# Order of blends, border rows, side work and weight buffers in a deformable-convolution and mixture-of-experts kernel

## The chip, the cores and the metric

The kernel runs on one core of a Trainium2 chip. The metric is the device time of one execution in microseconds (us); the time stated for a kernel is the median of its runs. The profile that the text reads is that of one execution.

## What is computed

The input is `x`, four images of 256 channels and 64 x 64 pixels, in float32. The reference normalises each pixel over its channels, and then applies three modulated deformable 3 x 3 convolutions, each with a ReLU. For every pixel and each of nine taps, a plain 3 x 3 convolution gives an offset (dy, dx) and a mask; the input is sampled at the shifted place by bilinear blending of four neighbours, and the samples are multiplied with a 256 x 256 weight per tap.

```python
om = lax.conv_general_dilated(x, w_off, ...) + b_off[None, :, None, None]
off = om[:, :2 * K].reshape(B, K, 2, H, W)
mask = jax.nn.sigmoid(om[:, 2 * K:])
...
sampled = _bilinear(x, ys, xs) * mask[:, None]
out = jnp.einsum('bikhw,oik->bohw', sampled, wk) + b[None, :, None, None]
```

The result is added to `x`. Each of the 4 x 4096 pixels is then a token of 256 values. A token is normalised, a gate picks two of eight experts, and each expert is a two-layer network (256 to 512, GELU, 512 to 256) with biases. The two experts' results, weighted by the gate, are added to the token.

## The kernel before

**Tiling.** An image is cut into eight blocks of 512 pixels (eight rows of 64). A stage is one layer of one image; `self.stages` in `run` lists the twelve stages in a fixed order, chosen so that, but for two places, a stage does not need the one just before it. `main_block` walks one block: nine taps (`k`), and for each tap two pairs of 128-pixel groups (`t0`).

**Main path of a pair.** `samples` issues, for each of the two groups, an indirect gather from a table in DRAM (L503, on POOL, that is GpSimd) into a tile `g` of `self.gat`. One gathered row per pixel holds the four neighbours. VectorE (DVE in the profile) blends the two columns (L509, 128 x 512), then the two rows (L514, 128 x 256, into a tile `s`, of which there are eight), and ScalarE (ACT) scales the result by mask and weights (L517). `turn` works `LAG` = 2 pairs behind: four TensorE (PE) transposes (L532) and an ACT copy out of PSUM (L535). `finish` follows one tap behind that: the matmuls with the tap's weights (L555). After the ninth tap ACT writes the block (L577), for layers 0 and 1 into a window `win` of ten rows (eight and a border row on each side), for layer 2 into `r`.

**Side work.** Python generators hold the rest: `store_table` writes a window's rows into the DRAM table of the next layer; `off_block` computes offsets and masks of a block (PE matmuls L357 over the window, then some twelve small DVE instructions, L395 and after, that make the gather's indices and the blend's factors); `pre_block` normalises the next image; `tokens` forms, stores and normalises tokens and ranks the experts. `aside` puts a generator into a list once for each of its steps; `step(k)`, called after each tap, runs as many entries from the list's front as will empty it by the end of the block. Border rows that lie outside of the image are zeroed by memsets when a window is taken (L290, L292).

**Experts.** Three lanes (`routes`, `tiles`, `sums`) run beside the taps at a set pace (`Group.pace`; 5, 5, 2, 1.5 taps for one expert step). `expert` yields after each piece: first the bias addition of the step before (`products`, L892 on DVE, `y`) and transposes of 256 gathered tokens; then the first products and GELU (`ph` L856, L866); then `fetch_next` and the second products (`py` L874). `fetch` issues an indirect load of an expert's weights (L800, `w`, 1.18 MB: 128 x 2308 float32) into one of the tiles of `self.w`, and two of tokens (L812, `zt`), all on POOL. If the same buffer already holds the right weights, the row index lies out of bounds and nothing is loaded; `Group.order` therefore gives each buffer its own run of consecutive tiles. After the last tap the lanes are drained (`drain`).

**Order.** Each engine works its queue in order. The framework's scheduler sorts the instructions at build time, by readiness and by the order in which the program makes them. `with self.after(x)` forbids that what is made inside goes ahead of `x` on the same engine. `self.last` is the newest row blend, `self.gathered` the newest gather.

Of the kernel before, what the change touches and what calls it, by code (L numbers as in the profile page):

```python
# [11 lines left out]
ALU = mybir.AluOpType  # L12
# [5 lines left out]
CC = C // P  # L18
# [4 lines left out]
NB = H * W // BLK  # L23
RPB = BLK // W
# [5 lines left out]
Q = 32  # L30
# [4 lines left out]
FT_LOG = 8  # L35
FT = 1 << FT_LOG
FU = FT // P
GB = 10
LAG = 2
LEAST = 2.0**-30  # L40
WINN = CC * (RPB + 2) * W
# [41 lines left out]
class Group:  # L83


    def __init__(self, b, n0, n1):
        self.b, self.n0, self.n1 = b, n0, n1
        self.nm = f"{b}_{n0}"
        self.M = (n1 - n0) * TPB

        self.NF = 2 * self.M * P // FT + E - 1


        self.half = (self.NF + 1) // 2
        self.zt, self.acc, self.gy, self.sums, self.py = {}, [], [], [], None
        self.order = [s // 2 + s % 2 * self.half for s in range(self.NF)]


class Lane:
# [18 lines left out]
class Weave:  # L118
# [3 lines left out]
    def __init__(self, ctx, tc, ins, out):  # L122
        nc = self.nc = tc.nc
        self.tc = tc
        self.ins = ins
        self.x = ins["x"].rearrange("b (c p) h w -> b p c (h w)", p=P)
        self.out_v = out.rearrange("b (c p) h w -> b p c (h w)", p=P)
        self.B = self.x.shape[0]

        def pool(name, bufs, **kw):  # L130
            return ctx.enter_context(tc.tile_pool(name=name, bufs=bufs, **kw))

        self.cst = pool("cst", 1)
        self.dram = pool("dram", 1, space=bass.MemoryType.DRAM)
        self.wkp = pool("wkp", 1)
        self.plan = pool("plan", 19)
        self.win = pool("win", 3)
        self.wt = pool("wt", 2)
        self.small = pool("small", 1)
        self.big = pool("big", 2)  # L140
        self.ffn = pool("ffn", 2)
        self.rt = pool("rt", 1)
        self.rt2 = pool("rt2", 2)
        self.gyp = pool("gyp", 4)
        self.smT = pool("smT", 2)
        self.smp = pool("smp", 8)
        self.gat = pool("gat", GB)
        self.ps = pool("ps", 3, space=bass.MemoryType.PSUM)
        self.ps1 = pool("ps1", 1, space=bass.MemoryType.PSUM)

        self.routes, self.tiles, self.sums = Lane(), Lane(), Lane()
        self.side, self.plans_side = [], []
        self.last = self.gathered = self.turned = None
        self.starting, self.draining, self.later = True, False, []
        self.pend, self.pairs = None, []
# [125 lines left out]
    def window(self, n, nm, spare):  # L281

        if spare:
            if n % 2 == 0:
                self.spare = self.wt.tile([P, 2, WINN], F32, tag="wt", name=f"win_{nm}")
            w = self.spare[:, n % 2, :].rearrange("p (c r w) -> p c r w", c=CC, w=W)
        else:
            w = self.win.tile([P, CC, RPB + 2, W], F32, tag="win", name=f"win_{nm}")
        if n == 0:
            self.nc.vector.memset(w[:, :, 0, :], 0.0)  # L290
        if n == NB - 1:
            self.nc.vector.memset(w[:, :, RPB + 1, :], 0.0)  # L292
        return w

    def rows_done(self, l, b, n, wins):

        nc = self.nc
        w = wins[n]
        if n > 0:
            nc.scalar.copy(w[:, :, 0, :], wins[n - 1][:, :, RPB, :])  # L300
            nc.scalar.copy(wins[n - 1][:, :, RPB + 1, :], w[:, :, 1, :])  # L301
        if l > 0:
            self.aside(3, self.store_table(l, b, n, w))
        ready = [n - 1] * (n > 0) + [n] * (n == NB - 1)
        for m in ready:
            gen = self.off_block(l, b, m, wins[m])
            if self.starting and m >= NB // 2:

                self.later.append(gen)
            else:  # L310
                self.aside(6, gen, True)

    def store_table(self, l, b, n, w):

# [30 lines left out]
    def off_block(self, l, b, n, w):  # L345
# [4 lines left out]

        po = self.ps1.tile([P, BLK], F32, tag="po", name=f"po_{nm}")

        terms = [(ky, kx, c) for kx in (1, 0, 2) for ky in range(3) for c in range(CC)]
        for m, (ky, kx, c) in enumerate(terms):
            g = m % NQ
            x0, x1 = max(0, 1 - kx), min(W, W + 1 - kx)
            nc.tensor.matmul(  # L357
                po[g * Q : (g + 1) * Q, :].rearrange("q (r w) -> q r w", w=W)[:, :, x0:x1],
                lhsT=self.wo[l][:, 3 * ky + kx, c, :],
                rhs=w[:, c, ky : ky + RPB, x0 + kx - 1 : x1 + kx - 1],  # L360
                start=(m < NQ),
                stop=(m + NQ >= len(terms)),
                tile_position=(0, g * Q),
            )
# [26 lines left out]
        nc.scalar.copy(pos.rearrange("p (t k) d -> p t (k d)", k=K), pm[:, :, : 2 * K])  # L391
        yield
        yield
        with self.after(self.last):
            nc.vector.tensor_tensor(  # L395
                pos, pos, self.base[:, n].rearrange("p t k d -> p (t k) d"), ALU.add
            )
# [31 lines left out]
    def pre_block(self, b, n, wins, spare):  # L429
# [8 lines left out]
        for t0 in range(0, TPB, 2):  # L438
# [7 lines left out]
                    )  # L446
            nc.scalar.copy(h[:, t0 : t0 + 2, :], tp)
        yield
        rest = normalise(nc, self.small, h, h, EPS_C, nm)
        with self.after(self.last):  # L450
            next(rest)
# [42 lines left out]
    def samples(self, i, n, k, t0, plan):  # L494


        nc = self.nc
        idx, cf = plan
        ss = []
        for t in (t0, t0 + 1):  # L500
            j = t * K + k
            g = self.gat.tile([P, 2, 2, C], F32, tag="g", name=f"g_{i}_{n}_{j}")
            self.gathered = nc.gpsimd.indirect_dma_start(  # L503
                out=g.rearrange("p x s f -> p (x s f)"),
                out_offset=None,
                in_=self.table(*self.stages[i]),
                in_offset=bass.IndirectOffsetOnAxis(ap=idx[:, j : j + 1], axis=0),
            )
            nc.vector.scalar_tensor_tensor(  # L509
                g[:, :, 0, :], g[:, :, 1, :], cf[:, j, 0:1], g[:, :, 0, :],  # L510
                ALU.mult, ALU.add,
            )
            s = self.smp.tile([P, C], F32, tag="s", name=f"s_{i}_{n}_{j}")
            self.last = nc.vector.scalar_tensor_tensor(  # L514
                s, g[:, 1, 0, :], cf[:, j, 1:2], g[:, 0, 0, :], ALU.mult, ALU.add
            )
            nc.scalar.activation(s, s, AF.Copy, scale=cf[:, j, 2:3])  # L517
            ss.append(s)
        return ss
# [21 lines left out]
    def finish(self):  # L541
# [36 lines left out]
        if l < NL - 1:  # L578
            self.rows_done(l + 1, b, n, wins)
        else:  # L580
            self.aside(7, self.tokens(b, n, r))

# [2 lines left out]
    def tokens(self, b, n, r):  # L587
# [37 lines left out]
        nc.scalar.copy(lg, lp)  # L625
        nc.sync.dma_start(self.t_dram[b][n], tok)
        yield
        rest = normalise(nc, self.small, tok, z, EPS_T, nm)
        with self.after(self.last):
            mean = next(rest)  # L630
# [29 lines left out]
        )  # L660
        nc.scalar.activation(lg, lg, AF.Exp)
        yield
        sm = small("sm", (P, TPB))
        with self.after(self.last):
            nc.vector.tensor_reduce(sm, lg, AX.X, ALU.add)
# [24 lines left out]
    def route(self, grp):  # L690
# [60 lines left out]
        nc.vector.tensor_scalar(rows, ex, float(P), self.part, ALU.mult, ALU.add)  # L751
        same = small("same", (P, NF))
        nc.vector.tensor_tensor(same[:, 1:], ex[:, 1:], ex[:, : NF - 1], ALU.is_equal)
        nc.vector.memset(same[:, 0 : grp.half + 1 : grp.half], 0.0)
        nc.vector.scalar_tensor_tensor(rows, same, float(E * P), rows, ALU.mult, ALU.add)
        nc.vector.tensor_copy(grp.wrow, rows)

# [32 lines left out]
    def fetch(self, grp, step):  # L790

        if self.w is None:
            self.w = [
                self.wt.tile([P, 2, WINN], F32, tag="wt", name=f"w_{i}").rearrange(
                    "p a b -> p (a b)"
                )
                for i in range(2)
            ]
        f = grp.order[step]
        self.nc.gpsimd.indirect_dma_start(  # L800
            out=self.w[step % 2][:, : W1N + W2N],
            out_offset=None,
            in_=self.ins["W"],
            in_offset=bass.IndirectOffsetOnAxis(ap=grp.wrow[:, f : f + 1], axis=0),
# [20 lines left out]
    def expert(self, grp, step):  # L825

        nc = self.nc
        if step == 0:
            self.fetch(grp, 0)
            yield  # L830
        self.products(grp)
        f = grp.order[step]
        nm = f"{grp.nm}_{f}"
        w = self.w[step % 2]
        w1, w2 = w[:, :W1N], w[:, W1N : W1N + W2N]
        zt = grp.zt.pop(step)
        tp = self.ps.tile([P, CC, FT], F32, tag="tp", name=f"ftp_{nm}")
# [6 lines left out]
        nc.scalar.copy(zT, tp)  # L844
        yield

        beside = not self.draining
        if not beside:
            self.fetch_next(grp, step)
        hT = []  # L850
        for h0 in range(0, HC, 2):
            ph = self.ps1.tile([P, 2, FT], F32, tag="ph", name=f"ph_{nm}_{h0}")
# [13 lines left out]
                nc.scalar.activation(ht[:, h, :], ph[:, h, :], AF.Gelu, bias=w1[:, k : k + 1])  # L866
            hT.append(ht)
        yield
        if beside:
            self.fetch_next(grp, step)  # L870
        py = self.ps1.tile([P, FU, C], F32, tag="py", name=f"py_{nm}")
        for u in range(FU):
            for h in range(HC):
# [127 lines left out]
    def step(self, k):  # L1001

        for side in (self.plans_side, self.side):
            for _ in range(-(-len(side) // (K - k))):
                next(side.pop(0), None)

    def after(self, newest):

# [26 lines left out]
    def run(self):  # L1035
# [36 lines left out]
        for i, (l, b) in enumerate(self.stages):  # L1072
            wins, pre = {}, {}
            for n in range(NB):
                for gen in self.later[:2]:
                    self.aside(6, gen, True)
                self.later = self.later[2:]
                self.main_block(i, n, wins)
                if i in beside:
                    self.aside(5, self.pre_block(beside[i], n, pre, i == 0))  # L1080
            if i + 1 == len(self.stages) or self.stages[i + 1] == (l + 1, b):
                while self.pairs:
                    self.turn()
# [52 lines left out]
```

## Time and profile before

| | before |
|---|---|
| median of 12 runs | 6803.03 us (6799.7 to 6810.58) |
| profiled execution: device time | 6791.98 us |
| profiled execution: span of the instructions | 6790.3 us |
| gathers L503 on POOL | 3456, mean 1055 ns |
| column blends L509 on DVE | 3456, mean 743 ns |
| row blends L514 on DVE | 3456, mean 483 ns |
| POOL waits for a row blend (free gather buffer) | 641.1 us |
| DVE waits for a transpose (free sample tile) | 448.5 us |
| DVE waits for a gather | 404.0 us |
| DVE waits for second products, most of it in the drain | 216.3 us |

How to read it: busy time is the union of an engine's instructions, and sequencer work (waits, issues) is not in it. In a timeline, a line gives the start, the duration, the engine, the source line, the operation, what is written from what, and how many were merged; in brackets stand the idle time of the engine ahead of it and who ended it. The chain of waits follows the work that ended last back through who released it.

### The profile page before, as it was taken

Reading aid. Unit: us, or ns where it says so; the run is one execution under the profiler, and the core shown is the slowest. Engines: PE = TensorE matmul, PEld = TensorE weight load, DVE = VectorE, ACT = ScalarE, POOL = GpSimd, SP = SyncE. Lnnn points to the kernel's source line nnn. Section 1 sums busy time; section 2 is a strip of 40 time slices with the busy share of each in tenths; the row PEclk is TensorE's granted clock in tenths of the full one; section 3 lists DMA queues with packets and bytes.
Section 4 is the critical chain, followed back from the end, with each engine's and each line's share of the span. In section 5 each row is a group of like instructions: output and inputs, shape, how many; then the busy total and the mean of one; then the engine's idle time right before and its main releaser. Section 6 shows DMA issues by size and latency. Waiting matters only on the chain.

```text
span 6790.3 us, 88985 instructions
## 1 busy us (share of the span) xinstructions
PE 6207.4 (91%) x26500; PEld 3519.1 (52%) x26500; DVE 4965.8 (73%) x11467; ACT 3280.0 (48%) x7141; POOL 4447.0 (65%) x4245
## 2 busy tenths in 40 slices
PE   7998888889999999999999999999998899988887
PEld 3443344444445555555554555555555566655665
DVE  7887778778999676678888777667878555687521
ACT  3554555555555445445554455545554444454322
POOL 4664766666667666666667777666666666677643
PEclk9999999999999999999999999999999999999998
DMA  8998999999999999999998999989998887899744
GB/s 292 350 352 302 364 352 371 358 348 388 383 396 352 332 355 333 325 337 351 348 366 307 359 359 381 322 326 340 353 347 311 296 291 272 293 353 326 247 137 125
DMA packets 800319, 2223.73 MB, mean 327 GB/s; under 512 B 104728, under 2 KB 302872, under 8 KB 794080
## 3 DMA queue, kind: packets, MB, share of 16 engines
q0 software_dynamic: 551200, 1947.35, 77.8%
q1 hardware_dynamic: 248640, 270.69, 11.7%
q8 instruction: 215, 3.52, 0.2%
q14 instruction: 264, 2.16, 0.1%
HBM read 2160.68 MB, written 196.40 MB: 347 GB/s over the span
## 4 chain that ended last, share of the span: by engine, by line
PE 71%; ACT 9%; DMA 7%; DVE 6%; issue 4%; POOL 3%; SPq 0%; ACTq 0%; DVEq 0%; POOLq 0%
PE acc L555 36%; PE tp L532 10%; PE py L874 7%; PE ph L856 7%; PE po L357 7%; DMA g<-tab,idx 5%; ACT sT L535 4%; ACT s L517 2%; DVE g L509 2%; DVE s L514 1%; POOL gy L915 1%; PE pm L371 1%; POOL g L503 1%; PE lp_tok L618 1%; PE ftp L840 1%
## 5 line engine op out<-in xcount | busy, mean ns | idle before, releaser
L503 POOL DMA_INDIRECT g<-tab,idx x3456 | 3646.4, 1055 | 1787.1 <-DVE s L514 641.1
L555 PE MATMUL acc<-sT,wk 128*128 128x512 f32 x6912 | 3387.8, 604 | 152.0 <-ACT sT L535 137.2
L509 DVE SCALAR_TENSOR_TENSOR g<-g,cf 128x512 f32<-128x512 f32 x3456 | 2560.7, 743 | 408.0 <-DMA g<-tab,idx 404.0
L514 DVE SCALAR_TENSOR_TENSOR s<-g,cf 128x256 f32<-128x256 f32 x3456 | 1661.8, 483 | 734.0 <-PE tp L532 448.5
L535 ACT COPY sT<-tp 128x512 f32<-128x512 f32 x1728 | 1001.1, 586 | 1830.8 <-PE tp L532 1826.1
L517 ACT ACTIVATE s<-s,cf 128x256 f32<-128x256 f32 x3456 | 1640.4, 508 | 434.5 <-DVE s L514 399.8
L555 PEld LDWEIGHTS acc<-sT,wk 128*128 128x128 f32 x6912 | 1160.7, 192 | 967.4 <-issue 656.2
L532 PEld LDWEIGHTS tp<-ident,s 128*128 128x128 f32 x6912 | 879.8, 143 | 1358.6 <-issue 653.1
L532 PE MATMUL tp<-ident,s 128*128 128x128 f32 x6912 | 1249.7, 281 | 196.0 <-ACT s L517 179.1
L856 PE MATMUL ph<-fzT,w 128*128 128x256 f32 x2608 | 681.8, 394 | 58.0 <-ACT fzT L844 34.4
L874 PE MATMUL py<-w,hT 128*128 128x256 f32 x2608 | 651.3, 388 | 31.7 <-ACT hT L866 26.5
L856 PEld LDWEIGHTS ph<-fzT,w 128*128 128x128 f32 x2608 | 481.9, 195 | 186.2 <-ACT fzT L844 61.3
L874 PEld LDWEIGHTS py<-w,hT 128*128 128x128 f32 x2608 | 473.7, 191 | 163.9 <-ACT hT L866 68.8
L866 ACT ACTIVATE hT<-ph,w 128x256 f32<-128x256 f32 x652 | 282.2, 471 | 452.6 <-PE ph L856 433.2
L812 POOL DMA_INDIRECT zt<-z,tok x326 | 337.1, 1034 | 157.1 <-issue 86.5
L357 PE MATMUL po<-win,wo 128*32 128x504 f32 (+1 forms) x2304 | 356.6, 597 | 5.3 <-ACT win L301 3.0
L800 POOL DMA_INDIRECT w<-in_W,wrow x163 | 178.8, 1097 | 269.0 <-issue 95.3
L915 POOL DMA_INDIRECT gy<-ys,slots x256 | 260.8, 1019 | 109.0 <-issue 64.6
L892 DVE TENSOR_TENSOR y<-py,w 128x512 f32<-128x512 f32 x163 | 111.6, 684 | 219.8 <-PE py L874 216.3
L930 DVE SCALAR_TENSOR_TENSOR ta<-gy,cw,ta 128x256 f32<-128x256 f32 x256 | 120.4, 480 | 130.2 <-DMA gy<-ys,slots 76.8
L357 PE MATMUL po<-win_pre,wo 128*32 128x504 f32 (+1 forms) x1152 | 184.8, 619 | 2.0 <-ACT om L366 2.0
L357 PEld LDWEIGHTS po<-win,wo 128*32 128x32 f32 x2304 | 73.0, 109 | 176.8 <-issue 141.9
(154 smaller groups left out, 2930.1 us busy)
## 6 DMA issues: line engine op xcount, KB each, us to landing
tab<-hv SPq DMA_DIRECT2D x512, 128.0 KB
g<-tab,idx POOLq DMA_INDIRECT x3456
ys<-y SPq DMA_DIRECT2D x163, 256.0 KB
tab<-h_pre SPq DMA_DIRECT2D x128, 256.0 KB
wk<-in_conv_w SPq DMA_DIRECT2D x99, 256.0 KB
xc_pre<-in_x SPq DMA_DIRECT2D x32, 512.0 KB
xr_tok<-in_x SPq DMA_DIRECT2D x32, 512.0 KB
t<-t_tok SPq DMA_DIRECT2D x32, 512.0 KB
```

The lines of the kernel that those rows point to most:

```text
L357: nc.tensor.matmul(po[g * Q : (g + 1) * Q, :].rearrange("q (r w) -> q r w", w=W)[:, :, x0:x1], lhsT=self.wo[l][:, 3 * ky + kx, c, :], rhs= ...
L503: self.gathered = nc.gpsimd.indirect_dma_start(out=g.rearrange("p x s f -> p (x s f)"), out_offset=None, in_=self.table(*self.stages[i]), ...
L509: nc.vector.scalar_tensor_tensor(g[:, :, 0, :], g[:, :, 1, :], cf[:, j, 0:1], g[:, :, 0, :], ALU.mult, ALU.add,)
L514: self.last = nc.vector.scalar_tensor_tensor(s, g[:, 1, 0, :], cf[:, j, 1:2], g[:, 0, 0, :], ALU.mult, ALU.add)
L517: nc.scalar.activation(s, s, AF.Copy, scale=cf[:, j, 2:3])
L532: self.turned = nc.tensor.transpose(tp[:, c, u * P : (u + 1) * P], ss[u][:, c * P : (c + 1) * P], self.ident)
L535: nc.scalar.copy(self.sT[:, :, t0 * P : (t0 + 2) * P], tp)
L555: nc.tensor.matmul(acc[:, o, :], lhsT=self.wk[k][:, c, o * P : (o + 1) * P], rhs=sT[:, c, :], start=(k == 0 and c == 0), stop=(k == K - 1 ...
L812: self.nc.gpsimd.indirect_dma_start(out=zt, out_offset=None, in_=grp.zd, in_offset=bass.IndirectOffsetOnAxis(ap=grp.tok[:, j : j + 1], axi ...
L856: nc.tensor.matmul(ph[:, h, :], lhsT=w1[:, o : o + P], rhs=zT[:, c, :], start=(c == 0), stop=(c == CC - 1),)
L874: nc.tensor.matmul(py[:, u, :], lhsT=hT[h // 2][:, h % 2, u * P : (u + 1) * P], rhs=w2[:, h * C : (h + 1) * C], start=(h == 0), stop=(h == ...
L915: self.nc.gpsimd.indirect_dma_start(out=g, out_offset=None, in_=self.ys[grp.i % 3], in_offset=bass.IndirectOffsetOnAxis(ap=grp.slots[:, i, ...
```

## The change

The two groups of a pair are now gathered and blended by columns first, then both by rows; a row blend may not go ahead of the pair's second column blend. A pair's first gather buffer is thus freed later, and there are nine gather buffers in place of ten. Windows are no longer zeroed: the border matmuls of the first and last block leave out the row outside of the image, and for the first block `ky` goes 1, 2, 0, so that the four starting matmuls still cover the whole block. Side work takes each generator at most once a tap where others are in the list, and an empty step (`pause`) stands ahead of the DVE part of `off_block`, `pre_block` and (twice) `tokens`. In an expert step the bias addition of the step before moves from the first piece to the third, right ahead of the second products; the fetch for the next step moves from the third piece to the second, where it was only in the drain; three weight buffers take turns, and the tiles are ordered in thirds.

```diff
-GB = 10
+GB = 9
...
-        self.half = (self.NF + 1) // 2
+        self.third = -(-self.NF // 3)
-        self.order = [s // 2 + s % 2 * self.half for s in range(self.NF)]
+        self.order = [s // 3 + s % 3 * self.third for s in range(self.NF)]
...
-        self.wt = pool("wt", 2)
+        self.wt = pool("wt", 3)
... window
-        if n == 0:
-            self.nc.vector.memset(w[:, :, 0, :], 0.0)
-        if n == NB - 1:
-            self.nc.vector.memset(w[:, :, RPB + 1, :], 0.0)
... rows_done, run
-                self.aside(6, gen, True)
+                self.aside(7, gen, True)
... off_block
-        terms = [(ky, kx, c) for kx in (1, 0, 2) for ky in range(3) for c in range(CC)]
+        top, low = int(n == 0), int(n == NB - 1)
+        kys = (1, 2, 0) if top else (0, 1, 2)
+        terms = [(ky, kx, c) for kx in (1, 0, 2) for ky in kys for c in range(CC)]
+            y0, y1 = top * (ky == 0), RPB - low * (ky == 2)
-                po[g * Q : (g + 1) * Q, :].rearrange("q (r w) -> q r w", w=W)[:, :, x0:x1],
+                po[g * Q : (g + 1) * Q, :].rearrange("q (r w) -> q r w", w=W)[:, y0:y1, x0:x1],
-                rhs=w[:, c, ky : ky + RPB, x0 + kx - 1 : x1 + kx - 1],
+                rhs=w[:, c, ky + y0 : ky + y1, x0 + kx - 1 : x1 + kx - 1],
... off_block, pre_block, tokens (twice), ahead of the DVE part
+        for _ in self.pause():
+            yield
... samples
-        ss = []
+        ss, gs = [], []
-            nc.vector.scalar_tensor_tensor(
+            newest = nc.vector.scalar_tensor_tensor(
                 g[:, :, 0, :], g[:, :, 1, :], cf[:, j, 0:1], g[:, :, 0, :],
                 ALU.mult, ALU.add,
             )
+            gs.append((j, g))
+        for j, g in gs:
             s = self.smp.tile([P, C], F32, tag="s", name=f"s_{i}_{n}_{j}")
-            self.last = nc.vector.scalar_tensor_tensor(
-                s, g[:, 1, 0, :], cf[:, j, 1:2], g[:, 0, 0, :], ALU.mult, ALU.add
-            )
+            with self.after(newest):
+                self.last = nc.vector.scalar_tensor_tensor(
+                    s, g[:, 1, 0, :], cf[:, j, 1:2], g[:, 0, 0, :], ALU.mult, ALU.add
+                )
... finish, run
-            self.aside(7, self.tokens(b, n, r))
+            self.aside(9, self.tokens(b, n, r))
-                    self.aside(5, self.pre_block(beside[i], n, pre, i == 0))
+                    self.aside(6, self.pre_block(beside[i], n, pre, i == 0))
... route
-        nc.vector.memset(same[:, 0 : grp.half + 1 : grp.half], 0.0)
+        nc.vector.memset(same[:, 0 : 2 * grp.third + 1 : grp.third], 0.0)
... fetch, expert
-            out=self.w[step % 2][:, : W1N + W2N],
+            out=self.w[step % 3][:, : W1N + W2N],
... expert, first piece
-        self.products(grp)
... second piece
-        beside = not self.draining
-        if not beside:
-            self.fetch_next(grp, step)
+        self.fetch_next(grp, step)
... third piece
-        if beside:
-            self.fetch_next(grp, step)
+        self.products(grp)
... step
         for side in (self.plans_side, self.side):
+            moved = []
             for _ in range(-(-len(side) // (K - k))):
-                next(side.pop(0), None)
+                i = next((i for i, gen in enumerate(side) if gen not in moved), 0)
+                moved.append(side.pop(i))
+                next(moved[-1], None)
+
+    def pause(self):
+        return range(0 if self.starting or self.draining else 1)
```

## The prediction

> **What bounds the kernel now.** I read the page first: engine shares and the chain of waits.
>
> ```profile
> PE 6207.4 (91%) x26500; PEld 3519.1 (52%) x26500; DVE 4965.8 (73%) x11467; ACT 3280.0 (48%) x7141; POOL 4447.0 (65%) x4245
> PE 71%; ACT 9%; DMA 7%; DVE 6%; issue 4%; POOL 3%; SPq 0%; ACTq 0%; DVEq 0%; POOLq 0%
> ```
>
> TensorE carries most of the chain, VectorE (DVE) 6%. An average hides stages, so I read the table by stretch next (columns: length; busy of PE, weight loads, DVE, ACT, POOL; clock; DMA share; GB/s).
>
> ```profile
> 400.00:1600.00 1200.00, 1071.57 (x4330) 489.21 (x4329) 926.61 (x1956) 601.22 (x1333) 772.04 (x734) 1.00 0.94 351
> 1600.00:2100.00 500.00, 461.67 (x1993) 246.95 (x1992) 477.56 (x1327) 267.67 (x585) 349.62 (x310) 0.97 1.00 381
> 2100.00:5200.00 3100.00, 2919.14 (x12500) 1662.51 (x12498) 2373.43 (x5302) 1595.34 (x3458) 2117.21 (x2013) 0.99 0.93 344
> 5200.00:6000.00 800.00, 748.51 (x3305) 493.04 (x3305) 488.67 (x1027) 364.57 (x785) 515.94 (x510) 0.97 0.84 292
> 6000.00:6400.00 400.00, 354.47 (x1438) 221.07 (x1436) 305.71 (x767) 184.85 (x386) 298.12 (x273) 0.96 0.90 325
> 6400.00:6790.00 390.00, 311.50 (x1389) 247.59 (x1388) 84.53 (x225) 88.59 (x197) 166.03 (x171) 0.89 0.45 137
> ```
>
> Only 1600 to 2100 is paced by DVE (478 of 500 us busy). From 2100 to 6000 TensorE is 94% busy. PE's idle time by stretch is 128, 38, 181, 51, 46 and 79 us: 523 us that could be won at all, plus 59 before 400.
>
> **Column blends first.** The timeline of DVE, stage 1600 to 2100, shows today's order and, once, by chance, the new one.
>
> ```profile
> 1599.91 0.75 DVE L509 SCALAR_TENSOR_TENSOR g<-g,cf 128x512 f32<-128x512 f32 x1
> 1600.79 0.48 DVE L514 SCALAR_TENSOR_TENSOR s<-g,cf 128x256 f32<-128x256 f32 x1
> 1601.19 0.75 DVE L509 SCALAR_TENSOR_TENSOR g<-g,cf 128x512 f32<-128x512 f32 x1
> 1602.07 0.49 DVE L514 SCALAR_TENSOR_TENSOR s<-g,cf 128x256 f32<-128x256 f32 x1
> 1602.48 0.74 DVE L509 SCALAR_TENSOR_TENSOR g<-g,cf 128x512 f32<-128x512 f32 x1
> ...
> 1618.00 1.39 DVE L509 SCALAR_TENSOR_TENSOR g<-g,cf 128x512 f32<-128x512 f32 x2
> 1619.31 0.87 DVE L514 SCALAR_TENSOR_TENSOR s<-g,cf 128x256 f32<-128x256 f32 x2
> 1620.11 0.18 DVE L654 TENSOR_TENSOR lg_tok<-lg_tok,rs_tok 128x32 f32<-128x32 f32 x1
> ```
>
> A pair takes 1602.48 - 1599.91 = 2.57 us when each row blend follows its own column blend (0.88 us start to start), and 1620.11 - 1618.00 = 2.11 when two column blends go first. Start to start, a column blend and an instruction that does not need it are 0.66 apart: 0.22 saved each time. Counted in the trace, 2462 of the 3456 column blends are followed directly by a row blend (the others have side work between): 2462 x 0.22 = 542 us of DVE. By stretch: 610, 103, 1274, 252 and 105 of them from 400 to 6400, or 134, 23, 280, 55 and 23 us.
>
> The rule that speaks against this is in the Trainium skill, "VectorE: DVE Perf Modes", section "The DRAIN you can't avoid": the next VectorE instruction waits until the pipe is empty, with or without a semaphore, so order should not matter and this edit would be worth 0. The rows above, 0.88 against 0.66, say that it matters here.
>
> How much reaches the end? DVE waits for TensorE's transposes to free a sample buffer for 123 us in 400 to 1600 and 291 us in 2100 to 5200: there it is ahead, and what it saves it mostly waits longer. The chain from 400 to 1600 has only 1.3% DVE but 14.7% ACT (copy and scaling of samples, 176 us). A pair is complete 0.46 us sooner, which ACT may use. I take 10 us there (from 60 won to 15 lost, since the scaling moves against the copy in ACT's queue) and 25 from 2100 to 5200 (from 90, half of PE's idle 181, to 30 lost). In 1600 to 2100 all 23 us lie where DVE paces; the gathers already run at 381 GB/s and 30 us from 4560 reached 412, so bytes allow 500 x (1 - 381/412) = 38. I take 15 (0 to 23).
>
> **No zeroed rows.** 24 memsets of 0.165 us go, and with them a wait of the DVE queue for an old window:
>
> ```profile
> 4526.53 0.17 DVE L290 MEMSET win<- 128x128 f32 x1 [14.70 <-PE po L357]
> 4500.00:4530.00 30.00, 28.25 (x122) 14.33 (x120) 11.67 (x23) 15.07 (x34) 13.27 (x14) 1.00 0.58 210
> 4530.00:4560.00 30.00, 29.65 (x130) 17.93 (x129) 27.34 (x58) 16.08 (x37) 22.63 (x23) 1.00 1.00 377
> ```
>
> The longest of them, 14.70 us of DVE, cost TensorE nothing: 28.25 of 30 us busy in it and 29.65 after it. Eight ready samples cover it. So 0 (with up to 10 if that cover is gone). The clipped matmuls drop 64 of 512 columns in 6 of 36 terms of 24 blocks: their rows differ by 13 ns (504 against 512 columns), so under 3 us. The four starting terms still write the whole block.
>
> **Side work one step a tap, and pauses.** They issue nothing new. They take away DVE's waits for ACT: position 57.2 us, softmax sum 53.8, statistics 44.7 and 5.9, 162 in all, in pieces of up to 8 us, which the same eight samples cover: 0 on the path, 15 at most. Cost: plans and tables come about a tap later (about 6 us), on the path only where a stage needs the one before it, twice: 0 to 12.
>
> **Late bias addition, third weight buffer.** Today the weight fetch for an expert step overwrites the buffer that the bias addition y of two steps earlier still reads. The timeline in the late stretch:
>
> ```profile
> 5867.41 0.75 DVE L509 SCALAR_TENSOR_TENSOR g<-g,cf 128x512 f32<-128x512 f32 x1 [4.15 <-DMA g<-tab,idx]
> 5874.68 0.69 DVE L892 TENSOR_TENSOR y<-py,w 128x512 f32<-128x512 f32 x1
> 5876.15 1.42 POOL L800 DMA_INDIRECT w<-in_W,wrow  x1 [3.40 <-ACT s L517]
> ```
>
> The profile names ACT as releaser of the fetch, but the wait that its sequencer sits in ends at 5875.4, as y does (5874.68 + 0.69), and so at nearly every step from 5260 to 6000. POOL stands still for 3.4 us, the gathers queue behind w and two zt, DVE waits 234 us in this stretch for gathers, and y stands behind those blends: a closed loop. From 5340 to 5400 the chain is gathers, issue, POOL and DVE, almost no PE. With three buffers w waits for the y of three steps earlier, long done; the loop opens, and PE (748.5 of 800) is next. I take 30 of its 51 idle us, 12 of 46 in 6000 to 6400 (same loop), and 18 of the 19.8 us that PE waits for w in the drain; each from 0 to its whole.
>
> The cost: y now stands right ahead of the second products that need its PSUM tile, behind the newest row blend; TensorE, and all queued behind py, waits if DVE is late. Today that wait is 2.5 us in all. Bounds: 0, and one pair, 2.57 us, for each of some 128 steps, 329. DVE is ahead of PE where this would hurt, so the low row: 0, with the 30 above as reserve. The y store moves with it in SP's queue; tables behind it are read a stage later: 0. The fetch (w and two zt, about 4 us of POOL) only moves ahead by a piece. Thirds give each of the five groups one more weight load: 1.18 MB at 412 GB/s is 2.9 us, 14 us of DMA in stretches at 0.84 to 0.93 share: 0 (up to 14).
>
> **Nine gather buffers, held longer.** POOL already waits 641 us for a release. A tap of four gathers takes about 5.9 us (TensorE's chain repeats from 1213.73 to 1219.66), so ten buffers turn round in 14.8 us and nine in 13.3, and the first row blend of a pair releases later by one column blend, 0.66. From 400 to 1600 DVE hardly waits for gathers, so there is spare: 0. From 5200 it waits 284 us. I take 10 lost; bounds 0 and 1195 us (5200 to 6400) x 10/9 - 1195 = 133.
>
> **Sum.** 10 + 25 + 15 + 30 + 12 + 18 - 10 = 100 won on the profiled 6791.98 us (span 6790.3): 6692. The median of the runs, 6803.03, lies 11 higher: 6703.
>
> **Rivals.**
> (1) Slower: the gathers decide. Nine buffers, held longer, turn too slowly wherever gathers are late, above all from 5200 to 6400. Half the bound (in part of the gathers only) is 67 lost, and the loop's 42, the 25 and the 10 are not won, since late gathers take them back; 15 + 18 stay: 6803 + 67 - 33 = 6837, from 6815 to 6900. It decides once DVE's wait for gathers grows past its 404 us by about 100. For: POOL's 641 us of waiting for releases. Against: the third buffer takes away the very thing that makes gathers late.
> (2) DVE's 542 us reach the end more fully: the ACT terms of the chain shrink as pairs complete together. Half of all PE idle before 6000 (128 + 38 + 181 + 51 = 398) plus the other terms (12 + 18 - 10): 199 + 20 = 219, 6584. For: the page's PE share is not its peak. On that, the Trainium skill ("Trainium Kernel Development and Optimization", Performance Expectations) says to judge TensorE by its weight loads, 52% here, not by matmul busy time; by that rule half of PE would be free and this rival the likeliest. The 14.70 us stall that left PE 94% busy speaks against it.
> (3) Nothing reaches the end: 6803, if DVE's savings are waited away and the late y eats what the loop gives.
>
> **Chances.** Forecast (6640 to 6775) 0.50; rival 2 (6480 to 6640) 0.20; rival 3 0.08; rival 1 0.22. Range 6560 to 6840: it leaves out about half of rival 2 and half of rival 1. The likeliest case's own range is 6640 to 6775. Runs of before spread by 0.16%, so 0.2% (14 us) is about what a measurement can tell: faster 0.70, same 0.08, slower 0.22.
>
> **What would show it.** Right: pairs of 2.11 us on DVE, its wait for transposes above 449 us, no memset of a window, no POOL stop of 2 to 5 us ahead of w from 5200, gathers' wait below 404 us, stretch 400 to 1600 little shorter. Wrong: column blends still 0.88 from their neighbour; POOL's wait for row blends well above 641 with DVE's for gathers above 500 (rival 1); TensorE waiting for y; or the stretches from 400 to 5200 shorter by over 100 us (rival 2).

## The result, and the profile after

The kernel after took 6913.08 us (median; 6899.69 to 6923.09), the kernel before in the same runs 6806.63 us: a ratio of 1.0157, 95% interval 1.0148 to 1.0166, so 106 us slower. The forecast was 6703, with 6560 to 6840 as its range. The profiled execution of after has a span of 6909.4 us. The page's engine shares and chain of waits:

```profile
PE 6262.3 (91%) x26500; PEld 3557.3 (51%) x26500; DVE 4820.2 (70%) x11443; ACT 3277.7 (47%) x7141; POOL 4752.5 (69%) x4245
PE 59%; DMA 16%; DVE 7%; ACT 7%; issue 6%; POOL 4%; SPq 0%; POOLq 0%; ACTq 0%; DVEq 0%
```

DVE did become 146 us less busy (4965.8 to 4820.2). But the chain's DMA share rose from 7% to 16%, and POOL became 306 us busier (4447.0 to 4752.5) with the same 4245 instructions. The waits of after (engine, line, tile, awaited; us in total, times, longest us) say where that is felt:

```profile
DVE g L512 <- DMA g<-tab,idx: 928.5, 769, 10.5
DVE s L520 <- PE tp L538: 563.0, 378, 13.2
POOL g L506 <- DVE s L520: 549.2, 699, 11.3
```

DVE's wait for gathers went from 404.0 us to 928.5. POOL, on the other hand, waits less than before for a row blend to free a buffer (641.1 to 549.2), which does not look like a shortage of buffers. The table by stretch (columns as in the prediction):

```profile
400.00:1600.00 1200.00, 1070.78 (x4257) 489.97 (x4257) 862.24 (x1881) 585.43 (x1299) 772.95 (x713) 0.98 0.92 342
1600.00:2100.00 500.00, 433.85 (x1762) 212.28 (x1761) 423.70 (x1159) 248.59 (x543) 363.26 (x284) 0.98 0.94 352
2100.00:5200.00 3100.00, 2913.94 (x12519) 1686.64 (x12519) 2309.81 (x5332) 1591.31 (x3454) 2288.43 (x2015) 0.99 0.93 344
5200.00:6000.00 800.00, 725.32 (x3136) 456.47 (x3136) 466.88 (x1057) 346.01 (x752) 539.96 (x487) 0.97 0.81 285
```

The stretch from 1600 to 2100 was the one that DVE paced (478 of 500 us busy, 381 GB/s). Now DVE is busy for 424 of 500 us, DMA moves 352 GB/s, and POOL is busier (363 against 350 us) with fewer instructions (284 against 310). Counted from one stage's first column blend to the next one's, the fourth stage grew most, from 461 to 513 us. Not all of that is the order's: with the old order of blends and all other edits (an experiment below) this stage takes 493.5 us, so the order has 20 of the 52. It takes 30 and 21 us more in the last two stages.

What lengthens POOL's work shows in its timeline of after, early in the kernel:

```profile
640.22 1.15 POOL L506 DMA_INDIRECT g<-tab,idx  x1 [0.30 <-DVE s L520]
641.67 1.03 POOL L506 DMA_INDIRECT g<-tab,idx  x1 [0.30 <-issue]
643.00 5.38 POOL L506 DMA_INDIRECT g<-tab,idx  x1 [0.30 <-DVE s L520]
648.68 1.20 POOL L506 DMA_INDIRECT g<-tab,idx  x1 [0.30 <-DVE s L520]
```

One gather takes 5.38 us on POOL where its neighbours take 1.0 to 1.2. DVE's timeline of after over the same time:

```profile
639.68 0.87 DVE L520 SCALAR_TENSOR_TENSOR s<-g,cf 128x256 f32<-128x256 f32 x2
640.47 1.41 DVE L512 SCALAR_TENSOR_TENSOR g<-g,cf 128x512 f32<-128x512 f32 x2
641.80 0.87 DVE L520 SCALAR_TENSOR_TENSOR s<-g,cf 128x256 f32<-128x256 f32 x2
642.59 1.41 DVE L512 SCALAR_TENSOR_TENSOR g<-g,cf 128x512 f32<-128x512 f32 x2
643.91 0.87 DVE L520 SCALAR_TENSOR_TENSOR s<-g,cf 128x256 f32<-128x256 f32 x2
644.71 1.41 DVE L512 SCALAR_TENSOR_TENSOR g<-g,cf 128x512 f32<-128x512 f32 x2
646.03 0.87 DVE L520 SCALAR_TENSOR_TENSOR s<-g,cf 128x256 f32<-128x256 f32 x2
646.82 1.45 DVE L512 SCALAR_TENSOR_TENSOR g<-g,cf 128x512 f32<-128x512 f32 x2
648.19 0.88 DVE L520 SCALAR_TENSOR_TENSOR s<-g,cf 128x256 f32<-128x256 f32 x2
651.98 0.75 DVE L512 SCALAR_TENSOR_TENSOR g<-g,cf 128x512 f32<-128x512 f32 x1 [2.91 <-DMA g<-tab,idx]
```

Each pair takes 2.12 us (642.59 to 644.71), and every line but the last begins before the one above it has ended: 643.91 lies ahead of 642.59 + 1.41 = 644.00. DVE is not idle at all until 649.07; then it stands until 651.98 for want of a gather. The gather that began at 643.00 ends at 648.38, after a pair (at 646.82) whose second column blend comes 0.04 us late (1.45 us in place of 1.41). In the order of before, 0.13 us of DVE lay idle between a column blend and its row blend (1599.91 + 0.75 = 1600.66, next start 1600.79).

Over the whole trace of after 58 gathers took more than 3 us on POOL, of before 9. DVE was idle for 6% and 0% of the time of these, and for 33% and 27% of the time of gathers under 1.1 us. All of them, in both kernels, began when DVE had been busy without a gap for over 2 us, and 25 of the 58 ended 0.6 to 0.95 us after that run had ended. But a run without a gap does not hold every gather: in the lines above, those at 640.22 and 641.67 pass. Of 970 gathers of after that began with DVE busy without a gap for their next 2 us, 58 took over 3 us; in before 9 of 468. What decides which of them is held is not known. The fourth stage of after has one of over 4 us in nearly every block, 60 to 74 us apart.

### The profile page after: what moved, and what is told of

Read it like the earlier page. It is cut to its first block, busy times and chain, and to the rows that moved or that the text cites. A ratio compares the mean times of both kernels' runs of the same rounds, so it can differ in the third digit from the quotient of the medians.

```text
span 6909.4 us, 89016 instructions
## 1 busy us (share of the span) xinstructions
PE 6262.3 (91%) x26500; PEld 3557.3 (51%) x26500; DVE 4820.2 (70%) x11443; ACT 3277.7 (47%) x7141; POOL 4752.5 (69%) x4245
## 4 chain that ended last, share of the span: by engine, by line
PE 59%; DMA 16%; DVE 7%; ACT 7%; issue 6%; POOL 4%; SPq 0%; POOLq 0%; ACTq 0%; DVEq 0%
PE acc L561 30%; DMA g<-tab,idx 12%; PE tp L538 9%; PE py L880 6%; PE po L356 6%; PE ph L863 5%; ACT sT L541 3%; DVE g L512 2%; POOL g L506 2%; DMA tab<-h_pre 2%; ACT s L523 2%; DVE s L520 2%; POOL zt L822 1%; POOL gy L921 1%; PE pm L370 1%
## 5 line engine op out<-in xcount | busy, mean ns | idle before, releaser
L506 POOL DMA_INDIRECT g<-tab,idx x3456 | 3891.1, 1126 | 1619.3 <-DVE s L520 549.2
L512 DVE SCALAR_TENSOR_TENSOR g<-g,cf 128x512 f32<-128x512 f32 x3456 | 2518.5, 745 | 935.4 <-DMA g<-tab,idx 928.5
L520 DVE SCALAR_TENSOR_TENSOR s<-g,cf 128x256 f32<-128x256 f32 x3456 | 1533.8, 479 | 571.5 <-PE tp L538 563.0
L523 ACT ACTIVATE s<-s,cf 128x256 f32<-128x256 f32 x3456 | 1574.5, 505 | 588.8 <-DVE s L520 585.6
L538 PEld LDWEIGHTS tp<-ident,s 128*128 128x128 f32 x6912 | 833.8, 143 | 1219.2 <-ACT s L523 698.4
L538 PE MATMUL tp<-ident,s 128*128 128x128 f32 x6912 | 1166.0, 282 | 294.3 <-ACT s L523 289.1
L863 PE MATMUL ph<-fzT,w 128*128 128x256 f32 x2608 | 648.2, 386 | 11.4 <-ACT hT L873 9.7
L880 PE MATMUL py<-w,hT 128*128 128x256 f32 x2608 | 624.5, 388 | 22.9 <-DVE y L898 12.9
L822 POOL DMA_INDIRECT zt<-z,tok x326 | 389.6, 1195 | 144.8 <-issue 66.1
L356 PE MATMUL po<-win,wo 128*32 128x504 f32 (+3 forms) x2304 | 372.2, 620 | 19.2 <-ACT win L297 15.5
L356 PE MATMUL po<-win_pre,wo 128*32 128x504 f32 (+3 forms) x1152 | 188.9, 598 | 1.0 <-ACT om L365 1.0
```

What stands on the lines that cost most here:

```text
L356: nc.tensor.matmul(po[g * Q : (g + 1) * Q, :].rearrange("q (r w) -> q r w", w=W)[:, y0:y1, x0:x1], lhsT=self.wo[l][:, 3 * ky + kx, c, :], ...
L506: self.gathered = nc.gpsimd.indirect_dma_start(out=g.rearrange("p x s f -> p (x s f)"), out_offset=None, in_=self.table(*self.stages[i]), ...
L512: newest = nc.vector.scalar_tensor_tensor(g[:, :, 0, :], g[:, :, 1, :], cf[:, j, 0:1], g[:, :, 0, :], ALU.mult, ALU.add,)
L520: self.last = nc.vector.scalar_tensor_tensor(s, g[:, 1, 0, :], cf[:, j, 1:2], g[:, 0, 0, :], ALU.mult, ALU.add)
L538: self.turned = nc.tensor.transpose(tp[:, c, u * P : (u + 1) * P], ss[u][:, c * P : (c + 1) * P], self.ident)
L822: self.nc.gpsimd.indirect_dma_start(out=zt, out_offset=None, in_=grp.zd, in_offset=bass.IndirectOffsetOnAxis(ap=grp.tok[:, j : j + 1], axi ...
```

## Experiments

Ratios are to the kernel before in the same runs. Six runs (the first four on one chip, the last two on another) fell to chips on which the kernel before took about 7630 us in place of 6800, so of those runs only ratios to the kernel before on the same chip are used. Where a ratio is turned into us, it is taken times 6803.

**Nine gather buffers alone.**

```diff
-GB = 10
+GB = 9
```

> The kernel before with nine gather buffers in place of ten, nothing else. Theory 1 (too few gather buffers, held too long, make gathers late): slower by 40 to 90 us (0.6 to 1.3%), VectorE's wait for gathers up from 404 us to 600 or more. Theory 2 (the new order of blends costs by itself, whatever the number of buffers): within 20 us. Theory 3 (the expert edits cost: late bias addition, earlier fetch, one more load per group): within 20 us.

Measured: 0.9999 (0.9979 to 1.0020). The ninth buffer costs nothing where the order is the old one.

**The new order of blends alone**, with ten and with nine buffers: the hunk of `samples`, nothing else.

> The kernel before with the column blends of a pair ahead of its row blends, ten gather buffers. Theory 1: the first buffer of a pair is freed one column blend later, worth half a buffer at most, against 0.2 us of VectorE saved per column blend; within 40 us, of either sign. Theory 2: slower by 60 to 120 us. Theory 3: faster by 10 to 50 us.

> The kernel before with columns first and nine gather buffers. Theory 1: slower by 80 to 150 us, more than the two single edits together, VectorE's wait for gathers above 800 us. Theory 2: the same as columns first with ten buffers, within 20 us. Theory 3: within 30 us of the kernel before.

Measured: 1.0060 (1.0034 to 1.0086) and 1.0048 (1.0032 to 1.0063). The order costs by itself, though less than theory 2 expected (41 and 33 us in place of 60 to 120; theory 1 had allowed 40 with ten buffers and expected 80 to 150 with nine), and no less with ten buffers than with nine. 65 and 62 gathers take over 3 us, against 9 in the run with nine buffers and the old order on the same chip.

**The kernel after with ten buffers** (y and o in one tile each, to make room).

> The changed kernel with ten gather buffers; the room comes from single buffers for the bias sums y and the output tiles o of the expert part. Theory 1: 50 to 120 us faster than the changed kernel (6913 us), so 6790 to 6860. Theories 2 and 3: 6880 to 6920.

Measured: 1.0121 (1.0079 to 1.0163): still slower, as theories 2 and 3 expected.

**The kernel after with the old order of blends**, nine buffers.

> The changed kernel with the old order of blends alone (each group gathered, blended by columns and then by rows), nine gather buffers. Theory 1 (late gathers from nine buffers held longer): it loses the hold but not the buffer, so it gets back half of the change's loss, 1.005 to 1.010 of the kernel before. Theory 2 (the new blend order costs by itself, by what it does to the queues): it gets most of it back, 0.995 to 1.004. Theory 3 (the expert edits cost): still 1.012 or more.

Measured: 0.9969 (0.9955 to 0.9983), 6781.62 us; DVE's wait for gathers is 401.7 us, 12 gathers take over 3 us. So within the change the order alone costs 1.0157 - 0.9969 = 0.0188, or 128 us, and it is what makes gathers late.

**Side work alone, and expert edits alone.** The first has the hunks of `step`, `pause` and the counts of `aside`; the second has those of `order`, `fetch`, `expert` and three weight buffers, with ten gather buffers (y and o in one tile each).

> The kernel before with the side work of the change alone (one step of a generator a tap, the pauses, the longer lists), ten gather buffers. Theories 1, 2 and 3: within 0.2% of the kernel before, since VectorE's waits that it takes away lie under TensorE's work. Theory 4 (side work that comes later or in other order costs): slower by 0.4 to 1%.

> The kernel before with the expert edits alone (three weight buffers and thirds, fetch in the second piece, bias addition in the third), ten gather buffers; y and o have one buffer each to make the room. Theories 1 and 2: faster by 0.3 to 0.8%, since the loop of fetch and bias addition from 5200 to 6400 opens. Theory 3: slower by 0.4 to 1%, with TensorE waiting for y or POOL still stopped ahead of w.

Measured: side work 0.9996 (0.9986 to 1.0006); expert edits 0.9862 (0.9846 to 0.9879), 6711.41 us, which beats both kernels and is more than any theory expected (0.3 to 0.8%). The DMA share of its chain of waits is 4%, against 7% before and 16% in after:

```profile
PE 77%; ACT 8%; DVE 6%; DMA 4%; issue 3%; POOL 1%; SPq 0%; ACTq 0%; DVEq 0%; POOLq 0%
```

**The kernel after with two weight buffers and halves, ten gather buffers.**

```diff
-GB = 9
+GB = 10
...
-        self.third = -(-self.NF // 3)
+        self.third = -(-self.NF // 2)
...
-        self.wt = pool("wt", 3)
+        self.wt = pool("wt", 2)
...
-            out=self.w[step % 3][:, : W1N + W2N],
+            out=self.w[step % 2][:, : W1N + W2N],
```

> The changed kernel with two weight buffers and halves again, and ten gather buffers (late bias addition and early fetch stay). Theory 1: 0.998 to 1.006 of the kernel before. Theory 2: 1.008 or more. Theory 3: the fetch now waits for a bias addition that comes later still, so the stretch with an expert step every 1.5 to 2 taps is longer than in any other kernel.

Measured: 1.0277 (1.0260 to 1.0294). DVE's wait for gathers stays at 987.5 us with ten buffers. A new wait of DVE's bias addition for the weight load, 235.2 us, shows that the late addition needs the third weight buffer.

At this point the buffers had fallen as a cause and the long gathers on POOL had been found. Two explanations were left: the run of blends without a gap (G), or that a pair's buffers are held until its second gather has landed, and come free together (H).

**One gap put back.** Of the pair's row blends, that of the second group goes first. It needs the column blend just ahead of it, so one gap a pair returns, while what is held stays as it is.

```diff
-        for j, g in gs:
+        for j, g in reversed(gs):
...
-                self.last = nc.vector.scalar_tensor_tensor(
+                newest = self.last = nc.vector.scalar_tensor_tensor(
...
-            ss.append(s)
+            ss.insert(0, s)
```

> The kernel after with one change: of a pair's two row blends, that of the second group goes first, so each pair has one blend that stands right behind the column blend it needs (a step of 0.88 us in place of 0.66), and what is held and how long stays as it is. Theory G (gathers starve on POOL while VectorE's blends run without a gap; 58 gathers took over 3 us in the kernel after, 9 before): fewer than 20 gathers over 3 us, POOL's gathers at 1.06 to 1.08 us in the mean, VectorE's wait for gathers 400 to 600 us, ratio to before 0.990 to 1.004. Theory H (a pair's buffers are held until the second gather has landed, and come free together): wait for gathers above 850 us, ratio 1.012 to 1.018, as the kernel after.

Measured: 1.0035 (1.0017 to 1.0052), 6822.50 us. Swapping a pair's two row blends brings back 83 of the 128 us. Gathers over 3 us fall from 58 to 8, DVE's wait for gathers from 928.5 to 581.8 us. The gathers' group on POOL (busy us, mean ns, idle ahead of it), first after:

```profile
L506 POOL DMA_INDIRECT g<-tab,idx x3456 | 3891.1, 1126 | 1619.3 <-DVE s L520 549.2
```

and with the one gap:

```profile
L506 POOL DMA_INDIRECT g<-tab,idx x3456 | 3735.2, 1081 | 1740.5 <-DVE s L520 701.1
```

With the old order it is 1057 ns. The ratio lies within what G expected, outside of what H did. About 45 us stay, with the mean between the two.

**The kernel after with the old order and ten buffers.**

> The kernel after with the old order of blends and ten gather buffers (y and o have one tile each, to make room). If the ninth buffer is what separated the old order with nine (ratio 0.997) from the expert edits alone with ten (0.986): ratio 0.984 to 0.988. If it is the side work and the border rows: 0.995 to 0.998.

Measured: 0.9971 (0.9959 to 0.9984), as with nine (0.9969): the buffer again costs nothing.

**The new order alone once more, ten buffers.**

> The kernel before with the column blends of a pair ahead of its row blends and nothing else, ten buffers; it ran once on a chip where all was slower, with a ratio of 1.006. Theories G and H: ratio 1.010 to 1.022, VectorE's wait for gathers above 800 us; by G, besides, over 45 gathers of more than 3 us on POOL. Theory T1 (too few buffers): 0.985 to 1.000, since there are ten.

Measured: 1.0067 (1.0050 to 1.0083), 46 us, below what either theory had expected (1.010 to 1.022); wait for gathers 936.3 us, 63 gathers over 3 us.

**Expert edits, with the new order and its one gap**, ten buffers.

> The kernel before with the expert edits (three weight buffers, late bias addition, early fetch), ten gather buffers, and column blends first but the second group's row blend ahead of the first's. Theory G: VectorE saves 0.22 us a pair and the gathers are not starved, so as good as the expert edits alone or better, ratio 0.982 to 0.988. Theory H: the longer hold costs most of what the new order cost, ratio 0.998 to 1.006.

Measured: 0.9941 (0.9924 to 0.9958), between what the two theories expected. The one-gap order loses 54 us to the old order in the same surroundings (0.9862), although only 7 gathers pass 3 us; their mean is 1091 ns against 1052.

**Eleven buffers, on the kernel before with the new order**, without and with the one gap (y and o in one tile each).

> The kernel before with column blends first and eleven gather buffers (y and o have one tile each, to make room); with ten it took 1.0067 of the kernel before. Theory H (what is left of the cost is that a buffer is out of use for about 2 us more of its turn of 15): one buffer more gives 1.4 us of that back, VectorE's wait for gathers falls from 936 us below 650 and the ratio to 0.985 to 0.998. Theory G (gathers starve on POOL while blends run without a gap): as many gathers over 3 us as with ten (63), wait for gathers above 750 us, ratio 1.000 to 1.007.

> As the run with columns first and eleven buffers, but the second group's row blend goes first, which leaves one gap a pair. Theories G and H both at work: fewer than 15 gathers over 3 us and, with the longer hold paid by the eleventh buffer, wait for gathers below 450 us and ratio 0.985 to 0.996; if it is no better than the run with the gapless order, starved gathers cost nothing where there are eleven buffers.

Measured: 1.0078 (1.0060 to 1.0095) without the gap, 0.9999 (0.9989 to 1.0008) with it. An eleventh buffer leaves the wait for gathers as it was (934.9 against 936.3 us), and 74 gathers pass 3 us; with the gap 8 do, and the wait is 532.0 us. That speaks against H as far as the number of buffers can show it: more buffers do not help, the gap does, by 54 us. The second run missed its own range, though: G and H together had been expected to give a wait below 450 us and 0.985 to 0.996, that is, a gain on the kernel before, and there is none.

**Which edit takes back what the experts win.** Expert edits with side work, and expert edits with border rows, both with the old order and ten buffers.

> Expert edits and side work (one step a tap, pauses) without the border rows' edit, old order of blends, ten buffers. Expert edits alone took 0.986 of before, with side work and border rows together 0.997. If the side work takes back what the expert edits win: 0.995 to 0.999. If the border rows' edit does: 0.984 to 0.988.

> Expert edits and border rows (no memsets, clipped matmuls), without the side work's edit, old order of blends, ten buffers. If the side work takes back what the expert edits win: 0.984 to 0.988. If the border rows' edit does: 0.995 to 0.999.

Measured: with side work 0.9957 (0.9940 to 0.9973), with border rows 0.9851 (0.9835 to 0.9868), 6706.78 us, the lowest time of all, though not clear of the expert edits alone (0.9846 to 0.9879). Side work, neutral by itself, costs 65 us here (0.9957 - 0.9862). One new wait is seen wherever the whole edit of the side work is in, as in the timeline of DVE with the old order and ten buffers (fourth stage):

```profile
1671.68 0.74 DVE L512 SCALAR_TENSOR_TENSOR g<-g,cf 128x512 f32<-128x512 f32 x1
1675.92 1.38 DVE L78 TENSOR_SCALAR z_tok<-t_tok,mv_tok,rs_tok 128x256 f32<-128x256 f32 x4 [3.50 <-DMA tab<-h_pre]
```

`z_tok` and `h_pre` are tiles of the same pool of two buffers (`big`). With the steps spread out, the normalised next image is still waiting for its store to the table when the tokens need the tile, and DVE's queue stands with all blends behind it: 12 times, 50.7 us in all in this kernel, 31.4 us with expert edits and side work, and nowhere in the kernels without side work. The fourth stage has 26.5 us more than without side work (495.5 against 469.0). The eleventh stage, which starts near 5085 us, shows another part: either edit alone shortens it (side work by 47 us, expert edits by 32), both together by 0. The same wait is there with side work alone (30.7 us, and the fourth stage 25 us longer), where the shorter eleventh stage pays for it; so the wait fits what the fourth stage loses and not the whole 65. Why the two edits cancel in the eleventh is open.

**The two halves of the side work**, each on top of expert edits and border rows.

> Expert edits and border rows (0.985 of before) with side work dealt one step a tap, and without the pauses. If the dealing is what takes back 65 us: ratio 0.994 to 0.998, stage 3 (the fourth image-layer) longer by 15 to 30 us. If the pauses do: 0.983 to 0.987.

> Expert edits and border rows with the pauses and their longer step counts, dealt as before (a generator may take two steps in one tap). If the dealing is what takes back 65 us: ratio 0.983 to 0.988. If the pauses do, since plans and tables come a tap later: 0.993 to 0.998.

Measured, on the second of the slower chips: dealing alone 1.0067 (1.0044 to 1.0089), pauses alone 0.9968 (0.9940 to 0.9996). Dealing alone lies above every range that was expected, and pauses alone in the range for the case that the pauses cost. But the common base (expert edits and border rows) was not run on that chip, so neither ratio tells what its half costs. What can be told is that dealing is the dearer half by 1% on the same chip, 20 us of it in the fourth stage; it shows the wait of `z_tok` too (9.8 us), the pauses do not.

## Why the prediction was wrong, step by step

The five parts can be put in a row, each step between two measured kernels that differ in that part alone (but y and o have one tile each in the first three rows, which the last two give back):

| step | ratio | us | forecast us |
|---|---|---|---|
| expert edits | 0.9862 | -94 | -60 (-117 to +329) |
| and border rows | 0.9851 | -7 | 0 |
| and side work | 0.9971 | +82 | 0 (-15 to +12) |
| and nine buffers | 0.9969 | -1 | +10 (0 to +133) |
| and column blends first | 1.0157 | +128 | -50 (-173 to +45) |
| sum (by the ratio) | | +107 | -100 |

**The step that failed is "Column blends first".** It took the 0.22 us between a column blend and its row blend as pure waste of DVE, and asked only how much of the 542 us reaches the end. Its marker came true: pairs of 2.12 us against 2.11 foretold, so the rows of before, and not the rule that order should not matter, were the ones to go by. (The section cited for that rule also says that an instruction which is not held starts earlier, which the prediction left out.) What it did not ask is who else uses that gap. POOL's gathers do: without it 58 of them are held up on POOL by some 2 to 6.6 us each, 70 ns in the mean of all gathers, and DVE then waits for them (928.5 us in place of 401.7 with the old order). In the stretch from 1600 to 2100, where DMA had moved 381 GB/s, it now moves 352. One gap a pair, put back, ends most of the long holds and returns 83 of the 128 us; that is what shows the cause, for this part. The prediction also had no term for the order from 5200 on, where the last two stages of after take 50 us more than with the old order. It had the figure to suspect the gathers: they took 1055 ns on POOL in the mean, but the shortest only 939.

The Trainium skill has a rule for this, in "SBUF — State Buffer", section "Who interferes with whom": a VectorE instruction with two inputs in SBUF contends with a GpSimd instruction that reads SBUF, since its second input comes through the read interface that the two engines share. The shared pair of ports is "an exclusive lock" there. The traces agree in kind: a blend reads two tiles of `g`, a gather reads its indices, and gathers are held over 3 us only while DVE runs without a gap. The same section reports that `tensor_tensor` did not stall a DMA, and infers that it takes only the read interface while descriptor generation needs the write interface. If that held for these blends and gathers, none would be held; 58 were. That it is this port, and not another thing of the two engines, no run here shows.

**The bounds failed too.** The loss was bounded by +15 and +30 us in the two long stretches and 0 in the DVE-paced one, which is about the fourth stage, where the order cost 20 us. A bound "0 to 23 won" excluded a loss without a reason.

**Rival 1** named the right symptom and side (gathers late, wait above 500 us; 6837 forecast, 6815 to 6900 as its range, 6913 came), but not the cause: its buffers cost -1 us, and its marker "POOL's wait for row blends well above 641" came out the other way, 549.2. Had that marker been read alone it would have cleared the gathers. **Rival 2** fell with the order: what DVE saved was more than lost again in waiting for gathers. Whether TensorE has half of its time free, as the rule it leaned on would have it, no run here tests.

**Expert edits** won 94 us and not 60, and the mechanism was only partly as described. TensorE's wait for weights (19.8 us) no longer appears among the waits of after, and the drain got 12 us shorter in after (24 with expert edits alone). But the loop did not open: in after, POOL still stands ahead of w between 5700 and 6100 us, as its timeline shows, and over the whole kernel POOL's idle time ahead of w is 260.0 us, against 269.0 before.

```profile
5759.64 1.05 POOL L810 DMA_INDIRECT w<-in_W,wrow  x1 [2.75 <-ACT s L523]
5779.95 1.05 POOL L810 DMA_INDIRECT w<-in_W,wrow  x1 [3.07 <-ACT sT L541]
```

Both start 0.88 us after a bias addition has ended (5758.76 and 5779.06). The prediction said that three buffers make w wait for a y "of three steps earlier, long done". Counted in pieces, y moved two later and the fetch one earlier, which uses up the three that a third buffer gives: the distance is two pieces, as before. The gain of expert edits alone lies, beside the 32 us in the stage after 5085 and the drain, in stages that were not in this edit's sum (13 and 17 us in the seventh and tenth, between 2980 and 5085). Which of late addition, early fetch and third buffer brings it was not taken apart. TensorE's wait for y stayed small, as said: 12.9 us against 2.5.

**Side work** was costed at nothing because eight sample buffers would cover DVE's short stops. It did remove the wait for the softmax sum (53.8 us to none), but the position's wait grew (57.2 to 72.2 us), and moving steps made two tiles of one pool live at once. The prediction followed queues, and not the buffers that the moved steps share. How much of the 82 us is that wait is not shown.

**Border rows and nine buffers** cost and won nothing measurable: the first as forecast, the second better than the 10 us lost of the forecast. The small term for clipped matmuls was mis-sized all the same: 13 ns is the difference that 8 columns make, 64 are dropped, and in after 12 of a block's 36 matmul records are clipped, 288 in all. By its own row that is 13 x 8 x 288 = 30 us of TensorE, not under 3.

Not settled: the order alone costs 46 us on the kernel before, but 128 on top of the other edits; and with one gap a pair back, 45 to 54 us remain in two of the settings, with gathers some 25 to 40 ns longer than in the old order. The cause of this rest is open. In both of these settings POOL waits longer for a row blend than with the old order (701.1 against 587.8 us, and 696.8 against 628.9), which is what H's longer hold would do; so H is excluded as the main cause, and not for the rest.

## What to carry to other kernels

A short idle gap of one engine may be time that another engine needs: before closing it, look in the trace at how long the other's instructions take beside a dense run and beside a loose one (here up to 7.5 us against 0.94). When a transfer is issued by an engine that can be held up, count its time on that engine, its longest as well as its mean. And when a step is moved, list the tiles whose buffers it shares with what it now runs beside, and count the distance from a buffer's last reader to its next writer in steps, before and after.

## What the runs showed of the hardware

- A gather's instruction on POOL, 0.94 us at the least, lasted up to 7.5 us in after and up to 9.1 us in the run with the new order alone, while VectorE ran without a gap; most gathers in such runs passed (all but 58 of 970 in after). One gap of about 0.13 us a pair brings those above 3 us down from 58 to 8.
- VectorE starts a 128 x 512 blend's independent successor 0.66 us after it, a dependent one 0.88 us after; four blends in a row in the new order overlap at their ends.
- The kernel before took about 6800 us on most chips and 7630 on two; in the six profiled runs there the mean granted clock was 0.94, where the others have 0.97 to 0.98.
